# Three changes of order in one transformer layer: exponentials before copies, a rotary turn over three slots, sums begun by copies

## The chip, the cores and the metric

The kernel runs on one core of one Trainium2 chip. The core has five engines that work side by side, each from its own queue and in the order of that queue: TensorE (PE) multiplies matrices and turns tiles, VectorE (DVE) and GpSimd (POOL) do element by element work, ScalarE (ACT) does activations and copies, and SyncE (SP) issues transfers. An instruction that waits for another engine's result holds up everything behind it in its own queue. The metric is device time in microseconds (us). The kernel before took 1428.4 us (median of three runs, 1426.82 to 1429.14). Two measurements of this kernel that differ by less than about 0.2% (2.9 us) can't be told apart.

## The reference, cut to what matters

The reference runs four layers, each a pre-norm attention and a feed-forward part that are both added to x (4 x 256 tokens, 512 features). The change is in layer 2 (L2), which has 32 query heads on 8 key heads of 128 features, and a feed-forward with a low-rank mixture of experts:

```
qkv = xn @ Wqkv.T                               # 32 query heads, 8 key heads, 8 value heads
xq, xk = rope(xq), rope(xk)                     # x1*c - x2*s, x1*s + x2*c over halves of 128
scores = where(causal, xq @ xk.T / sqrt(128), -1e30)
attn_output = (softmax(scores) @ xv) @ Wo.T
ffn = xn @ W_base.T + b_base + mixed_experts(xn) @ B_w.T * 2
x = x + attn_output + ffn
```

## The kernel before

Everything is float32. Layers 0 and 1 come first; `layers_2_and_3` then runs L2 and L3 from an order that is written out by hand. PE, DVE, ACT and POOL run in exactly that order; SP's transfers are placed by the tile framework.

**Tasks and slots.** The large products are cut into 2 x 2 blocks and multiplied with seven block products instead of eight (`seven`, table `SEVEN`: PSUM banks X, Y, Z, W, X, Z, W, named k = 0 to 6). Each block product is a task of four matmuls, and each task is one slot. `after(k, f)` puts f into the slot k later, where it is emitted behind that slot's task. PSUM has eight banks with one buffer each: S and U for scores, T and V for turned probabilities and values, and X, Y, Z, W for the tasks. So a task can only write into a bank when whoever reads the bank's last content is done. Tasks k = 4, 5, 6 add more products to the contents of X, Z and W, and so also wait for the readers of tasks 0, 2 and 3.

**Quads.** L2 goes through 16 quads of four heads. A quad's list holds (in this order) a key group in some quads (`key_tasks`, 7 tasks), the next quad's queries (`query_tasks`, 7 tasks) and the output product of the quad before (`output_tasks`, 7 tasks): 14 or 21 tasks. Quads 0 and 1 hold the two halves of the feed-forward's product, which `output_tasks` also does.

**Heads between the tasks.** `attend` gives each head h a step of m successive slots: 5, 5, 5 and 6 in a quad of 21 tasks, 3, 4, 3 and 4 in most quads of 14. `run` emits, for slot `at` of the step:

- at 0, ahead of the task: `scores(h)` on PE; behind it `masked(h)` on DVE, which adds the mask and finds the row minimum nm of the negated scores (L1725).
- at 1: `exponentials(h)`, four activations on ACT with row sums (L1741).
- at 2: `normalise(h)`, a reciprocal rs on DVE (L1752), and two multiplications on POOL (L1755).
- at m // 3, through `piece`: `transposes(h - 1)` on PE and `copies(h - 1)` on ACT (L1773, L1774), which bring the turned probabilities from PSUM into tiles q0 and q1. `piece` is emitted ahead of what is due in the slot.
- at 2m // 3: `values(h - 1)`, the product of q0 and q1 with the values (L1780, L1781).

So where m // 3 is 1 (m of 3, 4 or 5), slot 1 of a step gives ACT the copies of head h - 1 first and the exponentials of head h second.

**Quarters.** `quarters` gathers the four blocks of a query or key product. ACT copies X to u and Z to z, DVE adds Y to u (L1303), makes c = u + W (L1309), POOL adds z to c (L1310): c is the fourth quarter, (1, 1), and lies in SBUF while the other three lie in PSUM. `place` then gives each quarter to `rotary`: one product with cosines (L1376), two with sines on 64 partitions each (L1378), all three on DVE, and a sum on POOL (L1379). The fourth quarter comes last, 10 slots after the group's first task, that is in the second or third slot of the output tasks that follow.

**Sums.** `output_tasks` adds banks to x directly (L1412, `x_sb`) or, for tasks 0, 1 and 2, to shared sums `acc` (L1412), which are added to x once at the end of L2. POOL clears `acc` once with a memset (L1911). `biased` (L1895) adds the bias of the feed-forward to x, one row tile at a time, in slots 0 to 7 of quad 0.

**Behind L2.** The last quad also starts L3: x is normalised (`norm`, L1512 to L1520), turned on PE (L147), split into two parts (L1552, L1553) and multiplied (`whole`, L1561).

Of the kernel before, what the change touches and what calls it, by code (L numbers as in the profile page):

```python
# [26 lines left out]
ALU = mybir.AluOpType  # L27
# [3 lines left out]
P = 128  # L31
B, T, C = 4, 256, 512
NT = B * T // P
# [22 lines left out]
def block_stack(ctx: ExitStack, tc: tile.TileContext, d: dict, out: bass.AP):  # L56
    nc = tc.nc
# [16 lines left out]
    def bc(ap, axis, n):  # L74

        v = ap.unsqueeze(axis)
        shape = list(v.shape)
        shape[axis] = n
        return v.to_broadcast(shape)
# [1137 lines left out]
    def layers_2_and_3(w, late):  # L1217
# [8 lines left out]
        with ExitStack() as stack:  # L1226
# [15 lines left out]
            outs = []  # L1242
# [9 lines left out]
            def tile2(tag, bufs, name):  # L1252
                pool = rp if tag in ("kv", "u", "z", "c", "t2") else lp
                return pool.tile([P, 2, T], F32, tag=tag, name=name, bufs=bufs)


            acc = rp.tile([P, 2, 2, 2, T], F32, name="acc2")
# [5 lines left out]
            A = w.A  # L1263
# [8 lines left out]
            slot = [0]  # L1272
            due = {}

            def after(k, *fs):

                due.setdefault(slot[0] + k, []).extend(fs)
# [16 lines left out]
            def quarters(A, B, multiply, place, wait=7):  # L1294

                s = {}

                def steps(k, bank):
                    if k == 0:
                        s["u"] = tile2("u", 1, "u")  # L1300
                        after(1, lambda: nc.scalar.copy(s["u"], bank["X"]))
                    elif k == 1:
                        after(1, lambda: nc.vector.tensor_tensor(s["u"], s["u"], bank["Y"], ALU.add))  # L1303
                    elif k == 2:
                        s["z"] = tile2("z", 1, "z")
                        after(1, lambda: nc.scalar.copy(s["z"], bank["Z"]))
                    elif k == 3:
                        c = s["c"] = tile2("c", 1, "c22")
                        after(1, lambda: nc.vector.tensor_tensor(c, s["u"], bank["W"], ALU.add))  # L1309
                        after(2, lambda: nc.gpsimd.tensor_tensor(c, c, s["z"], ALU.add))  # L1310
                        after(wait, lambda: place((1, 1), c))

                def finish(tag, b):
                    if tag == "X":
                        after(1, lambda: place((0, 0), b))
                        return
                    after(1, lambda: nc.vector.tensor_tensor(b, b, s["u"], ALU.add))
                    after(2, lambda: place((0, 1) if tag == "Z" else (1, 0), b))

                return seven(A, B, multiply, steps, finish)  # L1320
# [48 lines left out]
                            skip_group_check=not start,  # L1369
                        )  # L1370

            def rotary(dst, src, tab):

                t2 = tile2("t2", 2, "t2")[:, 0 : src.shape[1], :]
                cos, sin = (bc(rope[:, tab + k, :], 1, src.shape[1]) for k in range(2))
                nc.vector.tensor_tensor(dst, src, cos, ALU.mult)  # L1376
                for at, of in ((slice(0, 64), slice(64, P)), (slice(64, P), slice(0, 64))):
                    nc.vector.tensor_tensor(t2[at], src[of], sin[of], ALU.mult)  # L1378
                after(1, lambda: nc.gpsimd.tensor_tensor(dst, dst, t2, ALU.add))  # L1379

            queries, kv = {}, {}

# [5 lines left out]
            def query_tasks(quad):  # L1388
                gp, hp, half = parts(quad)

                def place(c, src):
                    q = queries[quad, c] = tile2("q", 6, f"q2_{quad}_{c[0]}{c[1]}")
                    rotary(q, src, 0)

                return quarters(
                    lambda: A[half], lambda: w.sets["q", 2 * gp + hp].b, by_feature, place
                )

            def key_tasks(gp, half):
# [43 lines left out]
            class Layer3:  # L1443
# [193 lines left out]
                def biased(self, t):  # L1637
                    nc.gpsimd.tensor_tensor(x_sb[:, t, :], x_sb[:, t, :], self.row, ALU.add)
# [153 lines left out]
            def piece(h, k, m):  # L1792


                if h >= 1 and k == m // 3:
                    transposes(h - 1)
                    copies(h - 1)
                if h >= 1 and k == 2 * m // 3:
                    values(h - 1)
                    after(1, lambda: gathered(h - 1))  # L1800

            def spread(k, steps):

                for i, f in enumerate(steps):
                    after(k + i, f)
# [9 lines left out]
            def run(tasks):  # L1815

                for task in tasks:
                    h, at, m = beats.pop(slot[0], (None, 0, 0))
                    if h is not None and at == 0 and h < 4 * QUADS:
                        scores(h)  # L1820
                        after(0, lambda h=h: masked(h))
                        after(min(1, m - 1), lambda h=h: exponentials(h))
                        after(min(2, m - 1), lambda h=h: normalise(h))
                    task()
                    if h is not None:
                        piece(h, at, m)
                    while slot[0] in due:
                        for f in due.pop(slot[0]):
                            f()
                    slot[0] += 1  # L1830

            def sums_of(quad, eng=nc.gpsimd):
# [75 lines left out]
                    after(8 + 2 * g + i // 2, lambda t=4 * g + i: products(t))  # L1908
                after(10 + 2 * g, lambda g=g: turn_z(g))
            spread(6, outs[0].sums())  # L1910
            after(10, lambda: nc.gpsimd.memset(acc, 0.0))  # L1911
            run(key_tasks(0, 0) + query_tasks(0))

            def next_set():
# [48 lines left out]
            for quad in range(QUADS - 1):  # L1963
                gp, r = divmod(quad, 4)
                tasks = []
                if quad == 0:
                    tasks += key_tasks(0, 1)
                    after(len(tasks), next_set)
                    spread(0, [lambda t=t: biased(t) for t in range(NT)])
                if r >= 2 and gp < 3:  # L1970
                    tasks += key_tasks(gp + 1, r - 2)
                    if r == 3:
                        after(len(tasks), next_set)
                if quad == 1:
                    tasks += output_tasks(A[1], outs[0], 1, experts(1))
                    spread(len(tasks), outs[1].sums())
                    after(len(tasks), fetch_out)
                tasks += query_tasks(quad + 1)
                if quad == QUADS - 2:
                    after(len(tasks), l3.load)  # L1980
                    after(len(tasks) + 1, lambda: spread(1, l3.widened()))
                elif r % 2 == 0:
                    after(len(tasks), next_set)
                if quad == 0:
                    tasks += output_tasks(A[0], outs[0], 0, experts(0))
                else:
                    first = (len(tasks) + 7) // 4 if quad < QUADS - 2 else 1
                    spread(2 * first // 3 + 2, sums_of(quad - 1))
                    tasks += output_tasks(
                        attended.setdefault(quad - 1, {}),  # L1990
                        output_weights(quad - 1),
                        parts(quad - 1)[2],
                        last=quad == QUADS - 2,
                    )
                    if quad == QUADS - 3:

                        for i in range(4):
                            after(
                                4 + i,
                                lambda i=i: outs[8].sums(lambda k: tile2("kv", 13, f"wo2_8_{k}"))[i](),  # L2000
                            )
                    elif quad % 2 == 0 and quad < QUADS - 2:

                        k = quad // 2
                        spread(len(tasks), outs[k + 1].sums())
                        after(len(tasks), fetch_out)
                if quad == 1:
                    for k in range(4):
                        summed_raw(k, 42 * k)
                if quad == 4:  # L2010
                    spread(12, l3.integers())
                if quad == 11:
                    raws.close()
                    raw = raws.enter_context(tc.tile_pool(name="wq3s", bufs=1))
                    for s in range(2):
                        after(10 * s, lambda s=s, raw=raw: spread(4, w.layer3_sums(raw, s)))
                if quad == QUADS - 3:
                    after(0, raws.close)
                    attend(4 * quad, [0, 3, 6, 9, 12, 15, 18, 21, 24, 27, 31, 36, 41, 46])
                elif quad < QUADS - 3:  # L2020
                    attend(4 * quad, [len(tasks) * k // 4 for k in range(5)])
                run(tasks)


# [229 lines left out]
```

## Time and profile before

| what | value |
|---|---|
| median of three runs | 1428.4 us |
| the profiled execution's own time | 1424.28 us |
| its span in the profile | 1422.6 us, mean granted TensorE clock 0.988 |
| PE, DVE, ACT, POOL busy in the span | 96%, 63%, 36%, 52% |
| L2 in the span | from about 500 to 1300 us |
| PE busy from 500 to 1200 us | 96.6 to 100.0 us in each 100 |
| DVE, ACT, POOL busy from 800 to 900 us | 58.5, 34.3, 70.7 us in 100 |

The profile describes one execution, whose time (1424.28 us) is 4.1 us under the median of the runs. In a list of groups a row gives line, engine, operation, output and input, the count, the total and the mean time of one, and the idle time ahead of them with what ended it. In a timeline a row gives start and duration in us, engine, line and operation, and in brackets the idle time before it with what it waited for; `x8` after a matmul means eight records in a row, two for each float32 matmul. In the chain of work that ended last a row gives start, duration and the work that the end of the kernel is traced back through.

### The profile page before, as it was taken

To read this page: it belongs to the slowest core of one execution; us is meant where nothing else is said; L and a number is where in the kernel's file an instruction comes from. 1 tells how busy PE (TensorE), PEld (TensorE's weight loads), DVE (VectorE), ACT (ScalarE), POOL (GpSimd) and SP (SyncE) were. 2 spreads that over 40 slices of the span, in tenths; PEclk is the share of its full clock that TensorE was granted. 3 is DMA by queue.
4 is the path that set the end of the run, shared out by engine and by line. 5 is a ranking of instruction groups with operands and counts; after the bars stand their busy time and mean duration, and the time that the engine had idled before them with its cause. 6 is when DMAs were issued, how large, how long until landed. Compare 5 with 4: busy or idle time off the path is not lost.

```text
span 1422.6 us, 20817 instructions
## 1 busy us (share of the span) xinstructions
PE 1359.7 (96%) x7300; PEld 1066.8 (75%) x7300; DVE 899.1 (63%) x2370; ACT 509.8 (36%) x1333; POOL 738.0 (52%) x761
## 2 busy tenths in 40 slices
PE   7989999899999999999999999999999999989998
PEld 5656666588446677878887888888888788767887
DVE  6787777478926348635655756656557555858654
ACT  2344434387112213223232332333333333535430
POOL 3455546377733027555775956858659575210200
PEclk9999998999999999999999999999999999999999
DMA  5021223300510022011311203112222000302001
GB/s 194 2 58 35 45 45 76 86 0 3 156 61 15 1 82 75 0 45 34 105 41 60 67 16 100 60 45 64 68 63 86 30 16 16 118 1 112 0 1 60
DMA packets 50811, 76.15 MB, mean 54 GB/s; under 512 B 16475, under 2 KB 23798, under 8 KB 50322
## 3 DMA queue, kind: packets, MB, share of 16 engines
q1 hardware_dynamic: 49778, 73.77, 17.0%
q8 instruction: 58, 0.95, 0.3%
q10 hardware_dynamic: 816, 0.79, 0.2%
q0 software_dynamic: 112, 0.26, 0.1%
q14 instruction: 47, 0.39, 0.1%
HBM read 66.89 MB, written 7.91 MB: 53 GB/s over the span
## 4 chain that ended last, share of the span: by engine, by line
PE 79%; DVE 14%; ACT 2%; issue 2%; POOL 1%; DMA 1%; SPq 0%; DVEq 0%; ACTq 0%; POOLq 0%
PE m L1363 16%; PE m L1327 14%; PE dn L731 5%; PE gu L763 5%; PE s L1707 4%; PE av L1780 4%; PE m L1349 3%; PE m L1339 3%; PE half L278 3%; PE st L435 2%; PE s L1711 2%; PE l1o L1010 2%; DVE masked L389 2%; PE av L1781 2%; PE half L318 2%
## 5 line engine op out<-in xcount | busy, mean ns | idle before, releaser
L1755 POOL TENSOR_TENSOR p<-p,rs 128x512 f32<-128x512 f32 (+1 forms) x128 | 107.7, 863 | 242.3 <-DVE rs L1752 239.2
L1773 ACT COPY q<-pT 128x512 f32<-128x512 f32 x64 | 37.5, 586 | 280.1 <-PE pT L1764 280.1
L1741 ACT ACTIVATE p<-p,nm 128x256 f32<-128x256 f32 (+1 forms) x256 | 113.4, 451 | 54.4 <-DVE nm L1725 54.3
L1752 DVE RECIPROCAL rs<-sums 128x4 f32<-128x4 f32 x64 | 11.4, 178 | 178.1 <-ACT p L1741 177.8
L1327 PE MATMUL m<-xT,wq_b 128*128 128x256 f32 x448 | 105.6, 384 | 4.4 <-DVE x_sb L1577 3.0
L389 DVE CUSTOM_DVE_ANT_0 masked<-s,cmask 128x256 f32<-128x256 f32 (+1 forms) x256 | 89.8, 351 | 11.1 <-PE s L376 1.6
L1327 PEld LDWEIGHTS m<-xT,wq_b 128*128 128x128 f32 x448 | 83.1, 193 | 15.2 <-DVE x_sb L1577 3.4
L1310 POOL TENSOR_TENSOR c<-c,z 128x512 f32<-128x512 f32 x28 | 36.5, 1302 | 111.1 <-DVE c L1309 41.7
L1363 PE MATMUL m<-wo_b,o 128*128 128x256 f32 x384 | 90.2, 381 | 0.0
L449 POOL TENSOR_SCALAR_AFFINE_SELECT keys<-keys 128x256 f32<-128x256 f32 x128 | 57.0, 457 | 63.3 <-ACT keys L445 59.7
L1379 POOL TENSOR_TENSOR q<-q,t 128x512 f32<-128x512 f32 x64 | 85.3, 1334 | 6.1 <-DVE t L1378 6.1
L1378 DVE TENSOR_TENSOR t<-m,rope_sb 64x512 f32<-64x512 f32 (+1 forms) x144 | 86.3, 599 | 1.9
L1412 DVE TENSOR_TENSOR x_sb<-x_sb,m 128x512 f32<-128x512 f32 x82 | 54.5, 680 | 50.7 <-PE m L1363 40.7
L445 ACT ACTIVATE keys<-st 128x384 f32<-128x384 f32 x128 | 57.3, 488 | 75.3 <-PE st L435 75.3
L1725 DVE CUSTOM_DVE_ANT_0 p<-s,cmask 128x256 f32<-128x256 f32 (+1 forms) x256 | 76.2, 354 | 10.4 <-PE s L1707 8.0
L1363 PEld LDWEIGHTS m<-wo_b,o 128*128 128x128 f32 x384 | 70.8, 190 | 10.8 <-DVE t L1378 2.3
L1327 PE MATMUL m<-x_s,wq_t 128*128 128x256 f32 x320 | 75.5, 380 | 3.3 <-DVE x_sb L1412 2.2
L731 PE MATMUL dn<-wd,hT 128*128 128x512 f32 x176 | 76.4, 593 | 2.3 <-DVE sb L778 2.3
L783 POOL TENSOR_TENSOR sa<-sa,sb 128x1024 f32<-128x1024 f32 x22 | 62.2, 2832 | 30.3 <-DVE sb L778 30.3
L1789 ACT COPY o<-av 128x512 f32<-128x512 f32 x64 | 37.7, 589 | 89.1 <-PE av L1781 88.9
L1327 PEld LDWEIGHTS m<-x_s,wq_t 128*128 128x128 f32 x320 | 59.7, 190 | 12.7 <-DVE x_sb L1412 2.6
L1707 PE MATMUL s<-kv,q 128*128 128x256 f32 x256 | 66.4, 382 | 0.0
(329 smaller groups left out, 3483.3 us busy)
## 6 DMA issues: line engine op xcount, KB each, us to landing
wq_b<-in_wq SPq DMA_DIRECT2D x38, 256.0 KB
wo_b<-in_wo SPq DMA_DIRECT2D x32, 256.0 KB
raw<-in_wo SPq DMA_DIRECT2D x16, 512.0 KB
wkv_b<-in_wkv SPq DMA_DIRECT2D x16, 256.0 KB
wos_d<-wos_row SPq DMA_DIRECT2D x28, 128.0 KB
gate_q<-in_gate_q SPq DMA_DIRECT2D x11, 256.0 KB
up_q<-in_up_q SPq DMA_DIRECT2D x11, 256.0 KB
wq3s_b<-in_wq SPq DMA_DIRECT2D x8, 256.0 KB
```

Source lines behind the costliest of these rows:

```text
L389: nc.vector.tensor_tensor_reduce(out=ap.tile([P, T], F32, tag="masked", name="masked", bufs=1)[:, 0:n], in0=self.s[part][i][:, e, :], in1= ...
L731: nc.tensor.matmul(po, lhsT=hT[:, k, t * P : (t + 1) * P], rhs=wd[:, k, :], start=k == 0, stop=k == NBLK - 1,)
L763: nc.tensor.matmul(p[:, half], lhsT=w[:, g, :], rhs=x[half][:, g], start=k == 0, stop=k == 1,)
L783: nc.gpsimd.tensor_tensor(self.a, self.a, self.b, ALU.add)
L1327: nc.tensor.matmul(out[:, i, :], lhsT=b[:, c, i * P : (i + 1) * P], rhs=a[:, c, :], start=start and i == 0 and c == 0, stop=i == 1 and c == 1,
L1363: nc.tensor.matmul(out[:, t, :], lhsT=a[:, c, t * P : (t + 1) * P], rhs=b[:, c, :], start=start and t == 0 and c == 0, stop=t == 1 and c = ...
L1378: nc.vector.tensor_tensor(t2[at], src[of], sin[of], ALU.mult)
L1379: after(1, lambda: nc.gpsimd.tensor_tensor(dst, dst, t2, ALU.add))
L1707: nc.tensor.matmul(s1[:, i, :], lhsT=q[:, i, P:T], rhs=kt[:, 0, :], start=True, stop=True)
L1725: nc.vector.tensor_tensor_reduce(out=x[f"p{part}"][:, e, :], in0=x[f"s{part}"][:, e, :], in1=cmask if part else cmask[:, P : 2 * P], scale ...
L1741: nc.scalar.activation(p, p, AF.Exp, bias=x["nm"][:, part, e : e + 1], scale=-1.0, accum_out=x["sums"][:, part, e : e + 1],)
L1755: nc.gpsimd.tensor_tensor(p, p, bc(x["rs"][:, part, :], 2, n), ALU.mult)
```

## The change

1. In `run`, where a step's exponentials and its turn of the head before fall into the same slot 1 (`min(1, m - 1) == m // 3`, so m of 3, 4 and 5), `piece` is emitted after what is due in the slot, not ahead of it. ACT then gets the exponentials of head h before the copies of head h - 1. Steps of six keep their order.
2. The query groups call `quarters` with `wait=6` where it was 7, so that the fourth quarter's rotary turn begins one slot earlier, and `rotary` gets `pause=1` for that quarter: the product with cosines comes in slot 9 of the group, the two products with sines in slots 10 and 11, the sum on POOL in slot 12. Before, the three products came in slot 10 and the sum in slot 11. The tile c is taken one slot later, when it is first written. Key groups stay as they were.
3. The outputs of quads 0 and 1 (the feed-forward's) get `fresh=True`: the first addition to each of the four shared sums becomes a copy on ACT, and the memset on POOL goes.
4. `biased` moves from slots 0 to 7 of quad 0 to slots 4, 8, ... 32.

On PE the order of instructions stays the same, but for one place in the last quad, where the turn of normalised tile 1 comes ahead of the turn of head 61's probabilities. SP's transfers keep their contents, and some neighbours in the queue change places, among them the first `raw` tile of quad 1, which comes ahead of four `wo` blocks.

```diff
                     elif k == 3:
-                        c = s["c"] = tile2("c", 1, "c22")
-                        after(1, lambda: nc.vector.tensor_tensor(c, s["u"], bank["W"], ALU.add))
-                        after(2, lambda: nc.gpsimd.tensor_tensor(c, c, s["z"], ALU.add))
-                        after(wait, lambda: place((1, 1), c))
+
+                        def c22():
+                            s["c"] = tile2("c", 1, "c22")
+                            nc.vector.tensor_tensor(s["c"], s["u"], bank["W"], ALU.add)
+
+                        after(1, c22)
+                        after(2, lambda: nc.gpsimd.tensor_tensor(s["c"], s["c"], s["z"], ALU.add))
+                        after(wait, lambda: place((1, 1), s["c"]))
...
-            def rotary(dst, src, tab):
+            def rotary(dst, src, tab, pause=0):
...
+                def half(at, of):
+                    nc.vector.tensor_tensor(t2[at], src[of], sin[of], ALU.mult)
+
                 nc.vector.tensor_tensor(dst, src, cos, ALU.mult)
-                for at, of in ((slice(0, 64), slice(64, P)), (slice(64, P), slice(0, 64))):
-                    nc.vector.tensor_tensor(t2[at], src[of], sin[of], ALU.mult)
-                after(1, lambda: nc.gpsimd.tensor_tensor(dst, dst, t2, ALU.add))
+                low, high = slice(0, 64), slice(64, P)
+                for k, (at, of) in enumerate(((low, high), (high, low))):
+                    if pause:
+                        after((k + 1) * pause, lambda at=at, of=of: half(at, of))
+                    else:
+                        half(at, of)
+                after(1 + 2 * pause, lambda: nc.gpsimd.tensor_tensor(dst, dst, t2, ALU.add))
...
-                    rotary(q, src, 0)
+
+                    rotary(q, src, 0, int(c == (1, 1)))
 
                 return quarters(
-                    lambda: A[half], lambda: w.sets["q", 2 * gp + hp].b, by_feature, place
+                    lambda: A[half], lambda: w.sets["q", 2 * gp + hp].b, by_feature, place, 6
                 )
...
                     task()
-                    if h is not None:
+
+
+                    ready = h is not None and at == min(1, m - 1) == m // 3
+                    if h is not None and not ready:
                         piece(h, at, m)
                     while slot[0] in due:
                         for f in due.pop(slot[0]):
                             f()
+                    if ready:
+                        piece(h, at, m)
+                        while slot[0] in due:
+                            for f in due.pop(slot[0]):
+                                f()
                     slot[0] += 1
...
-            after(10, lambda: nc.gpsimd.memset(acc, 0.0))
...
-                    spread(0, [lambda t=t: biased(t) for t in range(NT)])
+                    for t in range(NT):
+                        after(4 + 4 * t, lambda t=t: biased(t))
...
-                    tasks += output_tasks(A[1], outs[0], 1, experts(1))
+                    tasks += output_tasks(A[1], outs[0], 1, experts(1), fresh=True)
...
-                    tasks += output_tasks(A[0], outs[0], 0, experts(0))
+                    tasks += output_tasks(A[0], outs[0], 0, experts(0), fresh=True)
```

## The prediction

> **What bounds the kernel now.** I read the busy table first, then the waits of L2 (540 to 1260 us), then the chain that ended last in the same stretch, then timelines at each place where the chain leaves PE. The waits (who waited for whom, us in total, times, longest) say that three engines queue up behind one another, while PE hardly waits:
>
> ```profile
> ACT q L1773 <- PE pT L1764: 275.0, 63, 9.8
> POOL p L1755 <- DVE rs L1752: 224.7, 52, 15.9
> DVE rs L1752 <- ACT p L1741: 177.8, 51, 5.9
> ...
> PE m L1363 <- DVE acc L1412: 4.5, 3, 2.2
> PE m L1327 <- DVE x_sb L1412: 2.2, 1, 2.2
> ```
>
> ACT sits before the copies until PE has turned the probabilities, although the exponentials behind those copies could run; DVE sits in rs until these exponentials are done; DVE's work behind rs is late. Most of it costs nothing, since PE is busy 96% of the span. What counts are the few places where PE waits in the end. The chain names them (start, us, what):
>
> ```profile
> 621.53 1.76 ACT p L1741 x8
> 623.41 1.26 DVE x_sb L1412 x2
> 624.72 1.99 PE m L1327 x8
> ...
> 735.53 1.76 ACT p L1741 x8
> 747.37 1.03 DVE q L1376
> 748.41 1.66 DVE t L1378
> 750.09 1.66 DVE t L1378
> 752.59 3.66 PE m L1363 x8
> ...
> 1229.52 1.76 ACT p L1741 x8
> 1232.06 1.45 DVE o_s L1070
> 1238.11 0.92 ACT xn L1520 x2
> ...
> 1244.67 1.28 ACT L1741
> 1245.96 1.86 ACT p L1741 x8
> ```
>
> The reader is to see the same start each time: exponentials, late, then DVE, then PE. The timelines give PE's wait: 2.19 us at 624.72 (for x_sb), 2.19 at 752.59, 2.08 at 1105.22 and 0.25 at 928.76 (all three for acc), 1.34 at 1230.13 (o_s), 0.89 at 1239.07 (xn), 1.84 at 1249.81 and 2.96 at 1264.64 (L3's start). At 752.59 eight matmul records take 3.66 us, where the same eight take 1.99 at 624.72: a slow clock.
>
> **What the Trainium skill says.** "TensorE: Matmul & The Clock Gate", Part 1: after an idle window the array runs at half clock, in windows of about 3.4 us that run freely. The trace agrees in kind: half clock from 752.75 for 3.41 us after the wait of 2.19, and twice more (from 1251.09 and 1264.75) after those of 1.84 and 2.96; the waits at 624.72 and 1105.22 drew none, so it is chance. "SBUF — State Buffer", section on the two sides: a DVE operation with two SBUF inputs and a GpSimd operation hold one port pair in turn. The trace agrees: a pair of t from c takes 2.68 us at 787.74 and 3.33 at 748.41 beside POOL work, a pair from PSUM 1.39. "ScalarE: Activation LUTs", "What ACT_TABLE_LOAD costs": a load is 1283 ns; the one at 1244.67 takes 1.28 us.
>
> **Exponentials first.** Nothing is added; rs comes earlier. In the step at 612.63, masked ends at 614.99, but the copies run at 620.67 and the exponentials from 621.42 to 623.2, so rs waits 5.90 us and x_sb comes at 623.41. Four exponentials take about 1.8 us from 0.5 after masked begins (587.02 to 587.56 in a step of six, which has this order already). So rs can run at about 616.2, x_sb no later than its own task (about 620), and PE's 2.19 us goes. The same shift takes the lag out of DVE in other steps: rs at 775.65 waited 4.17 us, and the three turns behind it ran late until the masked of 781.18, 2.0 us after its scores. Costed anew from PE's side: the tasks that feed the three turns end at 772.5, 774.9 and 777.7; a turn takes 0.7 + 1.4, a sum ahead of it 0.7. Turn 1 runs from 772.6 to 774.7, the sum and turn 2 from 775.0 to 777.7, the last sum ends at 778.6, and masked starts at about 779.0 when the scores (from 777.72) have their first half. Behind it on DVE come masked 1.2, turn 3 with 2.1, acc 0.6, q from c 0.9 to 1.2, rs 0.1, acc 0.6, acc 0.6 and one t of 1.34: 7.5 to 7.8, so the next masked could start at 786.8 and does at about 787.3, when its scores (786.16 to 787.6) are there, instead of 791.06.
>
> The price is the copies. In steps of three and four tasks values follow the turn by one task: turn over at 783.30, values at 784.87, q0 copied at 783.18 to 783.77, 1.1 us to spare. Exponentials finish 2.3 us after masked starts, so PE waits once masked starts later than about 1.4 us before the turn ends. With today's times that holds at the heads with masked at 791.06, 828.26, 965.70, 1002.76 and 1142.00 (0.7 to 0.9 us each) and 1222.09 (3.1 us), together 7 us; with the earlier times above at none. Steps of five have 2.8 us to spare. I take 0 and keep 7 for the range.
>
> **The rotary turn.** Same instructions, other places. In quads of 21 tasks the order was masked, acc, q, t, t, rs, acc, with 1.1 + 3.33 us of q and t (747.29 to 751.74) ahead of the acc that PE waits for. Now it is masked, q, acc, rs, acc, t, t, x_sb. From the masked that ended at 746.76: 1.1 + 0.6 + 0.1 + 0.6 gives 749.2, before PE's need at 750.4. So 2.19, 2.08 and 0.25 go, and with the first the slow clock, 3.66 - 1.99 = 1.67 us. What is late next: the x_sb of task 3 behind t, t, at 752.5 to 753.2, wanted by task 6 at about 753.4. That is 0.2 us; with the lag gone from this quad's DVE too (its rs at 737.32 had waited 4.0) it is over 2. In quads of 14 the t's stand one behind acc and one behind masked, with DVE ahead by then. POOL's last sum moves one slot; its order in the queue stays from quad 2 on, and the head that needs it comes half a quad later.
>
> **Sums by copies, bias later.** Four DVE adds of 0.68 us become four ACT copies of about 0.59 (L1422), the memset of 1.80 us goes. ACT is busy 24% there, and the second copy of quad 0 falls at about 591 where the add ran at 591.40. Eight sums of 1.27 us leave POOL's full stretch (548 to 567) for later gaps. PE waited 0.2 us for POOL at 548.5, before any of them. Price if a bias is late: DVE's x_sb waits up to 1.27 us for it; the sixth and seventh fall near 610 and 616, x_sb wants them at 612.8 and 620. I take 0. SP: a raw tile now stands ahead of four wo blocks and waits for POOL until about 616; the blocks come 12 us later than 604.88, but are first read a quad later, near 700. 0.
>
> **L2 to L3.** Since rs at 1231.30 waits 1.23 us no more and masked and o_s come about 1.3 us earlier, 1.34 at 1230.13 goes; the statistics behind it come earlier, so 0.89 at 1239.07 goes. Against it, head 61's copies now stand behind the table load and head 62's exponentials on ACT. They would come at about 1244.2, and values, wanted at about 1244.2, wait about 0.6; and the split behind them (L1552) is 1 us later relative to the exponentials, which still leaves the 1.84 at 1249.81 about 1.0. Net there 0, both ends -1.5 and +2. The 2.96 stays: it is DVE's own row of sums.
>
> **Sum**, against the profiled 1424.28 us: 2.19 + 2.19 + 2.08 + 0.25 = 6.7; slow clock 1.7; transition 2.2; 10.6, and 0.4 for an even chance of half of the other slow window at 1251. 11 us: 1413.3. Taken from the median of the runs, 4.1 us higher: 1417.4.
>
> **Rivals.** (a) Part only: stalls behind exponentials go (2.19 + 2.2), but the t's, still beside POOL, hold acc or x_sb elsewhere: gain 4.4, 1424.0. For it: the 0.2 us above. Against: the lag that made it tight goes. (b) No change: another wait, PE on POOL's p or c, takes the place: 1428.4. For it: POOL is busy 71%. Against: p was done 2.4 us or more ahead of its turn in the short steps, except 1.1 at 1227.97, and moves earlier. (c) Slower: late copies. DVE stays late in the short steps, because its own work there (t's at double price, L3's nibbles near 792) and not rs is what delays masked. Then values wait at the six heads, 7 us, and the body's gain fails too: 1435. It decides from masked starting later than 1.4 us before the turn's end. Against: rs waits about 4 us one or two steps ahead of most of them, and that goes.
>
> **Numbers.** The full gain 0.66 (its own range 1412 to 1422), (a) 0.15, (b) 0.08, (c) 0.11. Measuring tells 0.2%, 2.9 us, from no change. Faster takes the first and most of (a): 0.80; same 0.09; slower 0.11. The range reaches down to all PE waits of the transition and slow clocks gone, about 17 us, and up to (b): 1411 to 1428.
>
> **What would show it.** rs's wait for the exponentials should fall from 177.8 us to under 60, the copies' wait for PE lose about what the exponentials now fill of it, and PE should wait for acc and x_sb under 1 us in L2. A half clock near 750 should be gone. I am wrong if values (L1780) wait for q0, if the masked of heads 19 and 23 still start 4.9 us after their scores, or if PE waits for POOL.

## The result and the profile after

The changed kernel took 1413.7 us (median of four runs, 1412.0 to 1415.1) beside 1428.8 us before (1426.8 to 1429.7): ratio 0.9905, 95% interval 0.9882 to 0.9928, 15.1 us faster. Measured again later, beside other versions, it took 1410.1 us (six runs): ratio 0.9869, interval 0.9841 to 0.9897. The forecast was 1417.4 us, 11 us faster.

The profiled execution took 1412.54 us, with a span of 1410.8 us. The lines of L2 stand lower in the file now: exponentials L1754, masked L1738, rs L1765, copies L1786 and L1787, values L1793, the adds to acc and x_sb L1425. The waits of L2 and L3's start again (who waited for whom, us in total, times, longest):

```profile
POOL p L1768 <- DVE rs L1765: 148.9, 43, 15.6
ACT q L1786 <- PE pT L1777: 118.8, 59, 4.6
ACT p L1754 <- DVE nm L1738: 108.0, 56, 5.0
...
DVE rs L1765 <- ACT p L1754: 14.4, 12, 1.2
...
PE m L1331 <- DVE x_sb L1590: 3.0, 1, 3.0
...
PE av L1793 <- ACT q L1787: 0.9, 1, 0.9
```

rs hardly waits for the exponentials any more: 14.4 us instead of 177.8. ACT's copies wait for the turn 118.8 us instead of 275.0, since the exponentials now run in a part of that time. ACT's idle time moved more than it went. It waits longer for the row minima (108.0 us instead of 51.6) and for the values that it copies (155.5 instead of 86.0), and between the scores of head 0 and those of head 63 it is idle for 437.5 us where it was idle for 464.4. What the change altered is which work comes first. No line says that PE waits for acc in L2. What PE still waits for behind head 0's scores lies at L3's start.

The chain that ended last (start, us, what) shows the places that the prediction listed. Head 0's scores start 5.1 us later in this execution than in the profile of before, for a reason that comes below, so the times can't be compared one to one:

```profile
621.55 1.73 PE m L1367 x8
623.28 1.73 PE m L1904 x8
...
625.66 3.46 PE m L1331 x16
...
750.16 3.46 PE m L1367 x16
...
1233.87 1.28 ACT L1754
...
1235.16 1.86 ACT p L1754 x8
...
1252.33 0.61 DVE x_sb L1590
...
1252.98 3.62 PE m L1331 x8
```

At 625.66 (before: 624.72) and at 752 (before: 752.59) PE follows on PE. Sixteen records take 3.46 us, so eight take 1.73 where the slow ones took 3.66. Then the chain stays on PE until 1232.4, where ACT's work on the normalised tile, the table load at 1233.87 and head 62's exponentials follow, and DVE's row at L3's start remains.

### The profile page after: what moved, and what is told of

It is laid out like the page before. It is cut to its first block, busy times and chain, and to the rows that moved or that the text cites. A ratio compares the mean times of both kernels' runs of the same rounds, so it can differ in the third digit from the quotient of the medians.

```text
span 1410.8 us, 20812 instructions
## 1 busy us (share of the span) xinstructions
PE 1359.0 (96%) x7300; PEld 1068.8 (76%) x7300; DVE 895.8 (63%) x2366; ACT 520.7 (37%) x1337; POOL 734.1 (52%) x760
## 4 chain that ended last, share of the span: by engine, by line
PE 84%; DVE 10%; ACT 2%; issue 1%; POOL 1%; DMA 1%; SPq 0%; DVEq 0%; ACTq 0%; POOLq 0%
PE m L1367 18%; PE m L1331 15%; PE dn L731 5%; PE gu L763 5%; PE s L1720 4%; PE av L1793 4%; PE m L1353 3%; PE m L1343 3%; PE half L278 3%; PE st L435 2%; PE s L1724 2%; PE av L1794 2%; PE l1o L1010 2%; DVE masked L389 2%; PE half L318 2%; PE half L343 1%
## 5 line engine op out<-in xcount | busy, mean ns | idle before, releaser
L1754 ACT ACTIVATE p<-p,nm 128x256 f32<-128x256 f32 (+1 forms) x256 | 113.2, 443 | 108.2 <-DVE nm L1738 108.0
L1425 DVE TENSOR_TENSOR x_sb<-x_sb,m 128x512 f32<-128x512 f32 x82 | 55.9, 685 | 82.4 <-PE m L1367 67.4
L1738 DVE CUSTOM_DVE_ANT_0 p<-s,cmask 128x256 f32<-128x256 f32 (+1 forms) x256 | 76.1, 353 | 45.9 <-PE s L1720 43.8
L1391 POOL TENSOR_TENSOR q<-q,t 128x512 f32<-128x512 f32 x64 | 82.3, 1287 | 31.5 <-DVE t L1382 28.2
L1786 ACT COPY q<-pT 128x512 f32<-128x512 f32 x64 | 37.5, 585 | 122.5 <-PE pT L1777 120.5
L1793 PE MATMUL av<-q,kv 128*128 128x512 f32 x128 | 65.5, 593 | 0.9 <-ACT q L1787 0.9
```

The lines of the kernel that those rows point to most:

```text
L1391: after(1 + 2 * pause, lambda: nc.gpsimd.tensor_tensor(dst, dst, t2, ALU.add))
L1738: nc.vector.tensor_tensor_reduce(out=x[f"p{part}"][:, e, :], in0=x[f"s{part}"][:, e, :], in1=cmask if part else cmask[:, P : 2 * P], scale ...
L1754: nc.scalar.activation(p, p, AF.Exp, bias=x["nm"][:, part, e : e + 1], scale=-1.0, accum_out=x["sums"][:, part, e : e + 1],)
L1793: nc.tensor.matmul(av, lhsT=v[:, 0:P], rhs=x["q0"], start=True, stop=False)
```

## The experiments

**How they are compared.** The time from the start of the kernel to the first scores of head 0 is spent in layers 0 and 1, which no version touches. It still ranged from 544.6 to 555.8 us over the profiled executions, and 43 runs of the kernel before, measured beside four of the versions, lie between 1420.2 and 1432.3 us. That is wider than the 0.2% given ahead of the prediction, so a few runs of each version can't decide a difference of a few us. Besides the run times I therefore read a stretch from each trace: from the start of head 0's scores (L1707 before, first group of four matmuls) to the start of head 63's, and from there to the end.

| version | median us | ratio to before, 95% interval | to head 0 | head 0 to 63 | 63 to end |
|---|---|---|---|---|---|
| before | 1428.8 | | 548.54 | 704.84 | 169.20 |
| changed, first time | 1413.7 | 0.9905 [0.9882, 0.9928] | 553.66 | 688.63 | 168.54 |
| changed, second time | 1410.1 | 0.9869 [0.9841, 0.9897] | 545.91 | 688.62 | 168.43 |
| exponentials only | 1411.1 | 0.9877 [0.9839, 0.9915] | 548.26 | 690.09 | 170.33 |
| rotary turn only | 1422.2 | 0.9965 [0.9949, 0.9981] | 549.83 | 698.72 | 168.85 |
| sums and biases only | 1428.9 | 0.9999 [0.9983, 1.0015] | 555.77 | 704.95 | 169.21 |
| exponentials and rotary turn | 1409.7 | 0.9879 [0.9847, 0.9910] | 549.13 | 688.64 | 168.63 |
| exponentials in head 14's step only | 1423.8 (one run) | | 549.09 | 703.65 | 169.35 |
| exponentials in steps of five only | 1413.7 (one run) | | 552.60 | 692.46 | 166.90 |
| changed, with three edits at L3's start | 1404.3 | 0.9840 [0.9811, 0.9869] | 544.57 | 689.15 | 165.19 |
| the same, head 62 as in the changed kernel | 1403.2 | 0.9841 [0.9805, 0.9876] | 553.41 | 688.64 | 165.19 |

The changed kernel's stretch came out as 688.63 and 688.62 in two executions whose starts differ by 7.75 us. The change is worth 16.2 us there and 0.7 behind it. The two medians, 15.1 and 18.6 us below before, lie on both sides of this. The last column has luck in it: besides one at the very end, it holds one window of half clock in most executions (some with a part of another), two with the exponentials only (from 1250.35 and 1311.79) and none in the last three rows, and such a window costs some 1.5 us. The last section says what brings it.

**Exponentials only.** Of the diff only `run` is taken:

```diff
+                    ready = h is not None and at == min(1, m - 1) == m // 3
-                    if h is not None:
+                    if h is not None and not ready:
                         piece(h, at, m)
...
+                    if ready:
+                        piece(h, at, m)
...
```

> Only the exponentials go ahead of the copies; rotary turn, sums and biases as before. Theory A, each part removes its own places as the prediction summed them: the waits at 624.72, 1230.13 and 1239.07 go, those at 752.59 and 1105.22 (for acc, behind two products with sines) stay: 4 to 5 us faster than before, ratio about 0.997. Theory B, one cause for most: DVE, held in rs by late exponentials, is late at 752.59 too (rs at 737.32 had waited 3.96 us there), so that this wait and the slow clock behind it go without any change to the rotary turn, while 1105.22 stays (rs waited only 0.73 us ahead of it): 10 to 13 us faster, ratio 0.991 to 0.993. Late copies (the rival that ended slower): values wait for q0 in short steps, no gain or slower than before.

The stretch shrank by 14.75 us, nine tenths of the whole. Theory A falls: 752.59 is gone without the rotary edit. Theory B has the right places, but more came than its 10 to 13 us; what it left out stands in the section on the prediction. DVE's timeline around 752.59, first before (start, us, engine, line, operation, idle time before it in brackets):

```profile
737.32 0.18 DVE L1752 RECIPROCAL rs<-sums 128x4 f32<-128x4 f32 x1 [3.96 <-ACT p L1741]
...
745.58 0.42 DVE L1725 CUSTOM_DVE_ANT_0 p<-s,cmask 128x256 f32<-128x256 f32 x1
...
748.41 3.33 DVE L1378 TENSOR_TENSOR t<-c,rope_sb 64x512 f32<-64x512 f32 x2
751.78 0.18 DVE L1752 RECIPROCAL rs<-sums 128x4 f32<-128x4 f32 x1
751.87 0.66 DVE L1412 TENSOR_TENSOR acc<-acc,m 128x512 f32<-128x512 f32 x1
```

Then the same place in this version:

```profile
739.11 0.42 DVE L1725 CUSTOM_DVE_ANT_0 p<-s,cmask 128x256 f32<-128x256 f32 x1
...
743.13 1.38 DVE L1378 TENSOR_TENSOR t<-c,rope_sb 64x512 f32<-64x512 f32 x2
744.55 0.18 DVE L1752 RECIPROCAL rs<-sums 128x4 f32<-128x4 f32 x1
744.64 0.66 DVE L1412 TENSOR_TENSOR acc<-acc,m 128x512 f32<-128x512 f32 x1
```

The products with sines stand ahead of rs and acc in both, but with q ahead of them they take 3.20 us here and 4.44 before: POOL has run out of work at 742.58 here, where before it worked on until 751.20. And masked starts 1.65 us after head 15's scores (737.46), where it started 4.22 us after them before (745.58 after 741.36), since rs of the step ahead no longer waits 3.96 us. acc is done at 745.3, that is 7.8 us after these scores and not 11.2, and PE's task that needs its bank starts 8.9 us after them, at 746.33, without a wait. At the other place the gain is partial, and the waits of this version name it:

```profile
DVE rs L1752 <- ACT p L1741: 14.7, 15, 1.2
...
PE av L1780 <- ACT q L1774: 0.9, 1, 0.9
PE m L1363 <- DVE acc L1412: 0.8, 1, 0.8
```

The 2.08 us at 1105.22 became 0.82, because rs had waited only 0.73 us ahead of it and two products with sines take 3.33 us beside POOL. The rival that ended slower is nearly absent: values wait by 0.9 us at head 61, and at 1211.06 PE loses another 0.36 us to copies that come late for the weight load of values.

**Rotary turn only.** The edits of `quarters`, `rotary` and `query_tasks`, without the rest:

```diff
-                    rotary(q, src, 0)
+                    rotary(q, src, 0, int(c == (1, 1)))
...
-                    lambda: A[half], lambda: w.sets["q", 2 * gp + hp].b, by_feature, place
+                    lambda: A[half], lambda: w.sets["q", 2 * gp + hp].b, by_feature, place, 6
```

> Only the fourth quarter's rotary turn of the queries over three slots. Theories A and B: the waits for acc at 752.59, 1105.22 and 928.76 go (4.5 us), with the first the slow clock behind it (1.7): 4.5 to 6.5 us faster, ratio 0.9955 to 0.997; the waits at 624.72 and at L3's start stay, rs still waits about 178 us for the exponentials. Rival, the products with sines hold up what comes behind them in a later slot as much as they did: within 2 us of before.

The stretch shrank by 6.12 us, the time by 0.35% (0.19 to 0.51). All three waits of PE for acc are gone, while ACT and DVE queue as before:

```profile
DVE rs L1764 <- ACT p L1753: 182.0, 46, 5.9
...
PE m L1331 <- DVE x_sb L1424: 2.2, 1, 2.2
```

So the edit does what the prediction said of it, and the x_sb that it named as late next costs something: PE loses 0.28 us at 754.69 and 0.38 at 1103.14, start to start, because x_sb now stands behind the products with sines. The two parts of this edit, the earlier start and the pauses, were not measured apart. But 14.75 + 6.12 = 20.9 us for the two alone, and 16.2 together: 4.7 us are counted in both. Either edit removes the wait at 752.59 with its slow clock (2.35 + 1.7), the 0.4 at 928.8 and at least 1.26 of the 2.24 at 1105.2: 5.7 us. Of the 1.0 us between, 0.66 are the two delays behind x_sb in the version with the rotary turn only; the rest I have not traced.

**Sums and biases only.**

```diff
-            after(10, lambda: nc.gpsimd.memset(acc, 0.0))
...
-                    spread(0, [lambda t=t: biased(t) for t in range(NT)])
+                    for t in range(NT):
+                        after(4 + 4 * t, lambda t=t: biased(t))
...
-                    tasks += output_tasks(A[1], outs[0], 1, experts(1))
+                    tasks += output_tasks(A[1], outs[0], 1, experts(1), fresh=True)
...
-                    tasks += output_tasks(A[0], outs[0], 0, experts(0))
+                    tasks += output_tasks(A[0], outs[0], 0, experts(0), fresh=True)
```

> Only the sums begun by copies, without the memset, and the biases spread over 32 slots. Theories A and B: no wait of PE that exists hangs on POOL or on these adds, so within 1.5 us of before, ratio 0.999 to 1.001, the waits at 624.72, 752.59 and 1105.22 as they were. Rival C, the relief of POOL and DVE in the first quads carries a part of the gain: 4 us faster or more. A loss of up to 1.3 us if a bias holds up x_sb.

704.95 against 704.84 us, ratio 0.9999: nothing. The waits of 2.4, 2.35 and 2.2 us stand at their places, moved as a whole by the late start.

**Exponentials and rotary turn**, without the sums and biases, as in the two diffs above.

> Exponentials and rotary turn as in the changed kernel, sums and biases as before. Theories A and B: within 1.5 us of the changed kernel, so 13 to 16 us faster than before, ratio 0.989 to 0.991. Rival C: at least 4 us less of a gain than the changed kernel has, ratio 0.993 or more.

688.64 us against the changed kernel's 688.63. Rival C falls: relief of POOL and DVE in the first quads carries nothing. Against exponentials only, the rotary edit adds 1.45 us, of which 0.98 is the rest of the wait at 1105.22 and 0.36 the loss at 1211.06.

**One step only.** The kernel before, with one step changed, to see whether a single late rs explains 752.59:

```diff
+                    ready = h == 14 and at == min(1, m - 1) == m // 3
```

> The kernel before, with exponentials ahead of copies in a single step, that of head 14, in which rs waited 3.96 us at 737.32. One cause (late exponentials hold DVE in rs, DVE brings acc late): the wait before PE's task at 752.59 goes although the rotary turn is the old one, and the slow clock behind it with it: 2.35 + 1.7 us; all other waits stay (2.35 at 624.7, 2.24 at 1105.2, 1.51, 1.05 and 2.00 at L3's start). From the scores of head 0 to those of head 63: 704.84 becomes 700.8 (within 0.5). The other theory, the rotary turn itself makes acc late there: 704.8 stays.

The wait went, the expected 700.8 us did not come: 703.65. DVE's timeline first:

```profile
736.16 0.18 DVE L1752 RECIPROCAL rs<-sums 128x4 f32<-128x4 f32 x1 [0.56 <-ACT p L1741]
...
748.50 2.36 DVE L1378 TENSOR_TENSOR t<-c,rope_sb 64x512 f32<-64x512 f32 x2
750.90 0.18 DVE L1752 RECIPROCAL rs<-sums 128x4 f32<-128x4 f32 x1
750.99 0.66 DVE L1412 TENSOR_TENSOR acc<-acc,m 128x512 f32<-128x512 f32 x1
```

rs waited 0.56 us instead of 3.96, acc was done at 751.65, and PE's task started at 752.22 right behind its forerunner. So one late rs, one step earlier, was the cause there. The rest of the saving was lost elsewhere. In this execution half clock followed two waits that had drawn none in the profile before (PE's timeline; the eight records took 1.99 us there):

```profile
625.26 2.94 PE L1327 MATMUL m<-x_s,wq_t 128*128 128x256 f32 x8 [2.19 <-DVE x_sb L1412]
```

Over all the records of the window that is 1.64 us behind this wait and 1.67 behind the one at 1103.1. 4.1 us saved and 3.3 lost leave 0.8; 1.2 was measured, of which 0.25 are two short stalls near 740 that went too.

**Steps of five only.** Exponentials first where m is 5, the old order in steps of three and four:

```diff
+                    ready = h is not None and m == 5 and at == 1
```

> Exponentials ahead of copies in steps of five slots only, rotary turn, sums and biases as before. If the gain comes where PE waited: the waits at 624.7 and 752.6 go with the slow clock (6.4 us), that at 1105.2 falls to about 1.0 as with all steps; at L3's start heads 60 and 61 (steps of three and four) keep the old order, so the 1.51 us at 1230.1 stays. From head 0's scores to head 63's about 694 to 697, where all steps gave 690.09. If the short steps matter in themselves (lag handed from step to step): 699 or more.

692.46 us where 694 to 697 were expected: 12.4 of the 14.75 us come from the quads of 21 tasks and head 62. The wait at 1230.1 stays (1.50), as expected, and with it that of 1.06 at the turn of a tile behind it. These two, less the 0.36 lost at 1211.06, make up nearly all of the 2.4 us that exponentials first in the steps of three and four slots add. So where the copies stand closest to their need, the new order gained nothing else.

**A version that goes further.** What PE still waits for lies at L3's start, where DVE is the bound. Three edits to the changed kernel (`blocks` now returns its four sums; the one at index 2 overwrites a block of the turned x and stays behind its last reader):

```diff
-                    ready = h is not None and at == min(1, m - 1) == m // 3
+                    ready = h is not None and h < 62 and at == min(1, m - 1) == m // 3
...
-                    after(2, lambda: nc.vector.tensor_tensor(x, x, b, ALU.add))
+                    after(1 if t < 4 else 2, lambda: nc.vector.tensor_tensor(x, x, b, ALU.add))
...
-            after(8, lambda: l3.blocks(0))
+            sums3 = []
+
+            def ahead():
+                sums3.extend(l3.blocks(0))
+                for i in (0, 1, 3):
+                    sums3[i]()
+
+            after(7, ahead)
+            after(8, lambda: sums3[2]())
```

> The changed kernel, with three edits at L3's start: heads 62 and 63 keep copies ahead of exponentials; the product of a tile of layer 3 is added to x directly behind its scaling, not a slot later; three of the four sums of blocks come a slot earlier on DVE, where it idled, the fourth stays. Theory: values no longer wait for the copies (1.05 us at 1237.8), PE's wait of 3.13 us at 1253.0 falls to under 1 and the half clock behind it (1.6) goes: 4 to 5.5 us faster than the changed kernel, from head 63's scores to the end 165 us instead of 168.5. Rival: DVE, the bound of that stretch, makes PE wait two or three tasks later instead: within 1.5 us of the changed kernel.

From head 63 to the end it takes 165.19 us, as expected, 3.24 less than the changed kernel measured beside it. On the way there it lost 0.5 us, so the two stretches give 2.7 us where 4 to 5.5 were expected. With the copies of head 61 first, values no longer wait, but PE waits for the last turned tile:

```profile
1231.19 0.63 PE L147 MATMUL lnT<-ident,xn 128*128 128x128 f32 x4 [1.84 <-DVE rs L1764]
```

So the order of head 62 was put back and only head 63 kept copies first (`h < 63`):

> As the version with three edits at L3's start, but head 62 has its exponentials ahead of the copies again, as in the changed kernel; head 63 keeps copies first. Theory: what that version lost on the way into L3 (PE's wait of 2.00 us for the last turned tile, where the changed kernel waits 1.05 and 0.45) comes back as these two, so head 0's scores to head 63's take 688.6 us, and from there to the end 165.2: 653.8 us in all against 657.1 of the changed kernel and 654.3 of the other version. Median 3 to 4 us under the changed kernel's, ratio to before 0.983 to 0.988. Rival, the order at head 63 needs that at head 62: over 655 us.

The two stretches sum to 853.83 us, and the changed kernel has 857.05. The expected parts, 688.6 and 165.2, came true; their sum is 853.8, and the sums in the expectation are all 200 us too low. PE's timeline at L3's start, first of the changed kernel (second execution), then of this version:

```profile
1245.22 3.48 PE L1331 MATMUL m<-xT,wq_b 128*128 128x256 f32 x8 [2.98 <-DVE x_sb L1590]
```

```profile
1249.85 1.99 PE L1331 MATMUL m<-xT,wq_b 128*128 128x256 f32 x8
...
1255.52 1.78 PE L1331 MATMUL m<-x_s,wq_t 128*128 128x256 f32 x7 [0.57 <-DVE x_sb L1590]
```

The wait of 2.98 us and the half clock behind it (3.48 against 1.99 us) are gone, and 0.57 us of wait comes two tasks later. The median is 1403.2 us. Its interval overlaps that of the changed kernel, so that it beats it rests on the stretches. About half of the 3.2 us hangs on the half clock: with the exponentials in steps of five only, the same wait drew none, and its last stretch took 166.90 us, 1.7 more than here. Both versions beat the kernel before.

## Why the prediction was right, point by point

**Exponentials first** was right in its mechanism, and in the changed kernel nothing of its price came in L2's short steps. masked of heads 18 and 19 start 1.2 and 1.1 us after their scores begin; the prediction had 1.3 and 1.1. Values wait once, at head 61, as the prediction had it for L3's start. The step's size failed in one term: it credited these exponentials with 2.19 us and the transition's 2.2, and took the masked that ended at 746.76 as given. It had noted itself that rs at 737.32 had waited 4.0. Carried on, that lag is the wait at 752.59 with its slow clock. This edit alone is worth 14.75 us, not the 4.8 that these two and the 0.4 of the other slow window make.

**The rotary turn** was sized well as a change by itself (6.2 forecast, 6.1 measured). But it was not the only way to remove what it was credited with. Beside the exponentials it is worth 1.45 us. The sum was not wrong by this, since each wait was counted once.

**Sums by copies, bias later**: 0 forecast, 0.1 us measured. Of the order in SP's queue the runs say nothing by itself; no wait of PE for a transfer appeared.

**L2 to L3** was right in kind and 0.9 us too careful: 2.2 forecast, with a new wait of values and a shorter one at 1249.81 taken to cancel. The waits of 1.51, 1.05 and 2.00 us, counted start to start, became 1.05 (values for head 61's copies, forecast 0.6) and 0.45 (the last turned tile, forecast 1.0), together 3.1 less. The wait that was to stay, 2.96 at L3's start, stayed.

**The sum.** 11 us were forecast, 16.2 measured in the stretch. Start to start, every gap above the median spacing of its kind of matmul counted, PE lost 18.8 us there before and loses 2.6 now. By terms: the four waits of L2 count 7.35 instead of 6.7, since a wait costs some 0.15 us beside what the view of waits shows; the slow clock 1.7, as forecast; the transition 3.1 instead of 2.2; the other slow window 1.0 instead of 0.4. The rest, some 3 us, the prediction put at nothing. More than half of it are pairs of stalls of 0.15 and 0.1 us at the first two matmuls of the task behind values, in seven places (581, 640, 690, 740, 868, 918 and 1042 us). The view of PE's waits shows none of them, but that of PE's weight loads (PEld) in the same window before has them, since the first load of such a task waits for DVE's products with sines to leave the bank:

```profile
PEld m L1363 <- DVE acc L1412: 6.6, 7, 2.6
PEld m L1363 <- DVE t L1378: 2.7, 7, 0.4
```

Both rows are gone in the changed kernel, and the second also with the exponentials only or in steps of five only. It still stands with the rotary turn only (2.8 us, 7 times). So DVE's lag cost PE in more places than the four that the prediction took. Of all terms this one was furthest off.

**What would show it** came true: rs's wait 14.4 us (under 60 forecast), PE's waits for acc and x_sb in L2 none, half clock near 750 none, masked of heads 19 and 23 1.1 and 1.3 us after their scores, PE never behind POOL but for 0.2 us of a weight load at head 0's scores, which stood there before too. None of the rivals took over: no other wait came in L2 (a), PE waited for neither p nor c (b), and the copies came in time but for head 61 (c). One reading was wrong: the prediction called it chance that the waits at 624.72 and 1105.22 drew no half clock; the last section shows what decided it.

## What to carry to other kernels

When an engine waits in order for another (here DVE in rs), look for what could already run on the other one but stands behind an operation that is itself waiting: putting the ready work first was worth nearly the whole change here, for one wait of 1.05 us at head 61. Follow a lag forward before giving a stall to the work that stands directly ahead of it: at 752.59 two products with sines were in the way, but a late rs 15 us earlier decided it. Read the waits of the weight loads beside those of the matmuls: short stalls showed only there. Where an untouched part of the kernel varies by more than the change is worth, compare a stretch of the trace that contains the change.

## What the runs showed of the hardware

- **Time without a change of code.** The way to head 0 took 544.6 to 555.8 us in identical code, with the granted TensorE clock as the visible difference: 13.7 us of it ran at half clock in the execution with 544.6 us and 47.8 us in that with 555.8. From the view of stretches, for the version with sums only and for the one with three edits at L3's start:

```profile
40.00:100.00 60.00, 55.23 (x384) 35.16 (x383) 42.85 (x202) 24.49 (x59) 28.28 (x50) 0.77 0.12 28
```

```profile
40.00:100.00 60.00, 53.39 (x414) 34.40 (x413) 45.27 (x213) 26.19 (x63) 31.31 (x56) 0.91 0.13 28
```

  The columns are the stretch, its length, the busy time of PE, weight loads, DVE, ACT and POOL with counts, then the granted clock (0.77 and 0.91), the share of transfers and GB/s. In 60 us the second got through 414 matmuls, the first through 384. Of 43 runs of the kernel before in one series, the nine fastest took 1420.2 to 1420.8 us at a mean clock of 0.991, and most of the others 1428 to 1430 at 0.981 to 0.983.
- **Whether a wait brings half clock depends on where it falls.** Every trace keeps the stretches in which PE ran at half clock. In each of the eleven traces all of them start on one grid of 3.413 us (to within 2 ns). The program doesn't set where the grid lies: counted from the start of the kernel, the first edge comes 0.2 to 3.3 us later, depending on the execution, and counted from head 0's scores, 1.6 to 3.0 us later. I cut PE's waits behind head 0's scores (start to start, 0.7 us or more) at the edges. Half clock came at the next edge after all 14 waits that had 2.00 us or more between two edges, after 3 of the 14 that had 1.8 to 2.0 us, and after none that had less. The bounds are read off these waits, not tested. So the wait of 2.35 us at 624.72 drew nothing before, where an edge at 623.04 cut it into 0.68 and 1.68 us. It drew half clock with head 14's step only, where it lay whole between the edges at 622.75 and 626.16. In all, half clock followed 8 of 15 waits of 2.0 to 2.4 us and 7 of 9 waits of 3.1 us at L3's start. For whoever writes the order, the draw of a wait of 2 to 3 us stays chance; one that is kept under 1.8 us drew none here. "TensorE: Matmul & The Clock Gate", Part 1, of the Trainium skill gives an idle window of about 3.4 us as what brings the slow clock. These waits are shorter, and each window that followed cost 1.4 to 1.8 us on top.
